# A clear of 96 columns behind each GpSimd scatter of edge columns, slots and node scores, in a two-layer graph transformer kernel

## The chip, the cores and the metric

The kernel runs on one core of one Trainium2 chip. The metric is the device time of one execution in microseconds, as the median of several runs. Three runs of the kernel before gave 2740.04, 2740.24 and 2740.77 us, a median of 2740.24 us.

## The reference

A graph of 3125 nodes with 256 features and 50,000 edges passes through two layers. Each layer adds a graph step, a token mixing step and a feed-forward step to the residual x. Cut to the steps that the change touches, in float32:

```python
# layer 0, graph step: weighted sum over the edges
support = layernorm(x) @ W                       # 3125 x 256
x += segment_sum(support[dst] * edge_weight[:, None], src, 3125) + bias   # plus linear attention

# layer 0, feed-forward: a shared network and 8 experts, two per node
x += gelu(xn @ W1s + b1s) @ W2s + b2s + sum_e gate[:, e] * expert_e(xn)

# layer 1: graph attention and linear attention, then 4 experts, whose gates come
# from a second graph attention over 32,768 edges given as another input
scores = mean_heads(layernorm(segment_softmax_sum(h[src2], dst2)))
x += sum_e softmax(top2(scores))[:, e] * (gelu(xn @ W1[e] + b1[e]) @ W2[e] + b2[e])
```

## The kernel before, in words

The nodes lie as 25 tiles of 125 rows. `self.x` holds the residual in SBUF throughout.

**Layer 0, graph step (`layer0_mix`).** The edges are turned into a dense adjacency matrix `adj` of 3125 by 3125 numbers in DRAM, and TensorE multiplies it with `sup`, the support. `adj` is zeroed by plain DMAs (`fill`, line 372). The edges are cut into 15 chunks of 128 rows and `WIDTHS` = 16, ten times 32, 24, 16, 8 and 7 columns, 391 columns in all. `edge_chunk` (line 322) computes on DVE the summed weight and the place of each edge of a chunk, and then issues one scatter a column (lines 350 to 355): an indirect DMA on GpSimd's queue, `scatter` at lines 56 to 60, which writes 128 single numbers to `adj`. Every scatter appears in the profile under line 58, so they are told apart by their tiles.

The product runs in eight runs of blocks of 125 rows of `adj` (`RUNS`, line 39: blocks 0-3, 4-7, 8-12, 13-16, 17-20, 21-22, 23 and 24). Each run first sees to it that the edge chunks that it needs have been issued (line 452), then loads its blocks into the tile `adjT`, of which five buffers exist (`load`, line 439, the DMAs at line 445, on SP's queue in an order written out by hand), and then, for each pair of node tiles, accumulates its blocks on TensorE (line 460) and adds the result to x on DVE (line 463). A pass of line 460 is one record of TensorE; each float32 product leaves two. Between the pairs, one step of a sort of the 32,768 edges of the last stage is taken (`next(sort, None)`, line 464); its work is on DVE and TensorE.

**Layer 0, feed-forward.** Each node's row of 264 numbers (features, two gates, two slots, its own number) is scattered twice into `slots` in DRAM, 50 scatters (lines 788 to 790). The shared network's layers follow (`hidden`, `output`), and then blocks of 256 slots are loaded (line 849) and sent through their experts.

**Layer 1, feed-forward.** The scores of each node for the second graph attention, five numbers a row in the tile `row`, are scattered into `starts` in DRAM, 25 scatters (lines 1685 and 1686). The tiles that come after, `y` among them (line 1706), lie in the memory of the pool that holds `row`. Then four experts run over seven chunks of nodes (lines 1724 to 1734), while GpSimd gathers the scores of the edges (`sources`, line 1696, gathers at line 51).

SP's queue within `layer0_mix` and DVE's within the last expert loop are ordered by hand; everything else is ordered by the framework's scheduler, which also sets the waits on semaphores.

Of the kernel before, what the change touches and what calls it, by code (L numbers as in the profile page):

```python
# [8 lines left out]
F32 = mybir.dt.float32  # L9
# [46 lines left out]
def scatter(nc, table, idx, rows, add=False):  # L56
    kw = {"compute_op": OP.add} if add else {}
    return nc.gpsimd.indirect_dma_start(  # L58
        out=table, out_offset=bass.IndirectOffsetOnAxis(ap=idx, axis=0),
        in_=rows, in_offset=None, **kw)  # L60


def move(queue, out, in_):


    for s in (slice(0, 112), slice(112, P)):
        queue.dma_start(out[s], in_[s])  # L67
# [7 lines left out]
def rows_of(table):  # L75
    return table.rearrange("(t p) d -> p t d", p=P)


def overlapping(ap, start, steps):

    return bass.AP(tensor=ap.tensor, offset=ap.offset + start,
                   ap=[list(ap.ap[0])] + [list(s) for s in steps])
# [6 lines left out]
class Kernel:  # L89
    def __init__(self, ctx, tc, a, out):  # L90
        self.tc, self.nc, self.a, self.out = tc, tc.nc, a, out
        self.const = ctx.enter_context(tc.tile_pool(name="const", bufs=1))
        self.dram = ctx.enter_context(tc.tile_pool(name="dram", bufs=1, space=DRAM))


    def constants(self):
        nc, a, c = self.nc, self.a, self.const
        self.x = c.tile([P, NT, D], F32, name="x")
        self.ident = c.tile([128, 128], F32, name="ident")
        make_identity(nc, self.ident)  # L100

        self.below = c.tile([128, 128], F32, name="below")
        nc.gpsimd.memset(self.below, 1.0)
        nc.gpsimd.affine_select(out=self.below, in_=self.below, compare_op=OP.is_gt, fill=0.0,
                                base=0, pattern=[[-1, 128]], channel_multiplier=1)

        self.above = c.tile([128, 128], F32, name="above")
        nc.gpsimd.memset(self.above, 1.0)
        nc.gpsimd.affine_select(out=self.above, in_=self.above, compare_op=OP.is_gt, fill=0.0,
                                base=0, pattern=[[1, 128]], channel_multiplier=-1)  # L110
        self.full = c.tile([128, 128], F32, name="full")
        nc.vector.memset(self.full, 1.0)

        self.spare = c.tile([128, 1], F32, name="spare")
        nc.gpsimd.iota(self.spare, pattern=[[0, 1]], base=N, channel_multiplier=1,
                       allow_small_or_imprecise_dtypes=True)
        self.node = c.tile([128, EC], F32, name="node")
        nc.gpsimd.iota(self.node, pattern=[[1, EC]], base=0, channel_multiplier=0,
                       allow_small_or_imprecise_dtypes=True)
        self.eps = c.tile([128, 1], F32, name="eps")  # L120
        nc.vector.memset(self.eps, LN_EPS)
        self.ones = c.tile([128, 1], F32, name="ones")
        nc.vector.memset(self.ones, 1.0)


        names = (("L0_ffn_b1s", 8), ("L0_ffn_b1p", 64), ("L1_ffn_b1", 16), ("L0_mix_g_pre", 2))
        total = sum(n for _, n in names)
        self.cols = c.tile([128, total], F32, name="cols")
        self.col_at = {}
        with self.tc.tile_pool(name="c_s", bufs=1) as sp, \  # L130
                self.tc.tile_pool(name="c_p", bufs=1, space=PSUM) as pp:
            st = sp.tile([total, 128], F32, name="c_st")
            r = 0
            for name, n in names:
                v = a[name]
                flat = bass.AP(tensor=v.tensor, offset=v.offset, ap=[[128, n], [1, 128]])
                nc.sync.dma_start(st[r:r + n, :], flat)
                self.col_at[name] = r
                r += n
            pt = pp.tile([128, total], F32, name="c_pt")  # L140
            nc.tensor.transpose(pt, st, self.ident[:total, :total])
            nc.vector.tensor_copy(self.cols, pt)
# [179 lines left out]
    def edge_chunk(self, pool, out, k, c, pieces):  # L322


        nc = self.nc
        e0 = 128 * sum(WIDTHS[:c])
        F, K = WIDTHS[c], HALO
        C, W = self.chunk_in[c]

        same = pool.tile([128, F + K, K], BF16, name="ch_same", bufs=1)  # L330
        nc.vector.tensor_tensor(same, C[:, :F + K, None].to_broadcast([128, F + K, K]),
                                overlapping(C, 1, [[1, F + K], [1, K]]), OP.is_equal)
        prod = pool.tile([128, F, K], F32, name="ch_prod", bufs=1)
        nc.vector.tensor_mul(prod, same[:, K:, :], overlapping(W, 1, [[1, F], [1, K]]))
        more = pool.tile([128, F], F32, name="ch_more")
        nc.vector.tensor_reduce(more, prod, AX.X, OP.add)
        wsum = out.tile([128, F], F32, name=f"ch_sum{c}")
        nc.vector.tensor_add(wsum, more, W[:, :F])

        dup = pool.tile([128, F], F32, name="ch_dup")  # L340
        flat = same.rearrange("p i k -> p (i k)")
        nc.vector.tensor_reduce(dup, overlapping(flat, K - 1, [[K, F], [K - 1, K]]), AX.X, OP.max)
        own = C[:, K:K + F]
        off = pool.tile([128, F], F32, name="ch_off")
        nc.vector.scalar_tensor_tensor(off, k[F], float(BEHIND + e0), own,
                                       op0=OP.add, op1=OP.subtract)
        nc.vector.scalar_tensor_tensor(off, dup, self.off, off, op0=OP.max, op1=OP.mult)
        place = out.tile([128, F], I32, name=f"ch_place{c}")
        nc.vector.tensor_add(place, off, own)
        for f in range(F):  # L350
            ins = scatter(nc, self.adj[:], place[:, f:f + 1], wsum[:, f:f + 1])
            self.tc.declare_no_dep(ins.ins, group="adj read", reason="blocks that are complete")
            for i in range(pieces, BEHIND // PIECE):
                self.tc.declare_no_dep(ins.ins, group=f"zeros {i}", reason="rows behind the chunk's")
            self.unordered("adj", ins)

    def layer0_mix(self):
        nc, tc, a = self.nc, self.tc, self.a
# [327 lines left out]
    def layer0_ffn(self):  # L686
        nc, tc, a = self.nc, self.tc, self.a
        NE, FC = 8, 8
        with ExitStack() as c:
# [98 lines left out]
            for t in range(NT):  # L788
                for i in range(2):
                    self.unordered("slots", scatter(nc, self.slots[:], abi[:, i, t:t + 1], rows[:, t, :]))  # L790

            gT = keep.tile([NE + 1, N], F32, name="gT")
            for t0, n in CHUNKS:
# [847 lines left out]
    def layer1_ffn(self):  # L1641
# [4 lines left out]
        with ExitStack() as c:  # L1646
# [18 lines left out]
            with tc.tile_pool(name="f1l", bufs=1) as lp:  # L1665
                rows = lp.tile([128, EC, 16], I32, name="s_back")
                nc.sync.dma_start(rows, self.sorted[:].rearrange("(p f) c -> p f c", p=128))
                nc.vector.tensor_copy(src, rows[:, :, 0])
                self.layernorm(lp, ps_a, "3", xT)


                ph = ps_a.tile([P, NT, 16], F32, name="ln_pt")
                for t in range(NT):
                    self.token_matmul(ph[:, t, :], xT, t, wgat)
                h = srow[:, :, 0:16]
                nc.vector.tensor_copy(h, ph)
                prod = lp.tile([P, NT, 16], F32, name="prod")
                row = lp.tile([P, NT, 5], F32, name="row0")
                nc.vector.memset(row, 1.0)
                for n, dest in (("att_src", srow[:, :, 16:20]), ("att_dst", row[:, :, 0:4])):  # L1680
                    nc.vector.tensor_mul(prod, h, vec[n][:, None, :].to_broadcast([P, NT, 16]))
                    nc.vector.tensor_reduce(dest, prod.rearrange("p t (h k) -> p t h k", h=4), AX.X, OP.add)
                move(nc.sync, rows_of(tabg[:]), srow)

                for t in range(NT):
                    self.unordered("starts", scatter(nc, self.starts[:], self.seg_at[:, 0, t:t + 1], row[:, t, :]))

                nc.vector.tensor_add(loop, srow[:, :, 16:20], row[:, :, 0:4])
                nc.vector.scalar_tensor_tensor(loop, loop, 0.2, loop, op0=OP.mult, op1=OP.max)
# [326 lines left out]
```

## Time and profile before

| What | Value |
|---|---|
| median of three runs | 2740.24 us |
| the profiled execution, its own time | 3120.83 us |
| its span | 3119.1 us |
| granted TensorE clock, mean | 0.843 |
| TensorE busy | 2254.7 us (72%) |
| DVE busy | 1500.3 us (48%) |
| ACT busy | 541.0 us (17%) |
| GpSimd busy | 1645.8 us (53%) |
| mean DMA traffic | 83 GB/s |

The profiled execution took 380.6 us longer than the median of the timed runs, so a duration in the profile may stand for less in a timed run. A group's line reads: line, engine, operation, output<-inputs, count, then busy time and mean nanoseconds of one, then the idle time of its engine just before it and what ended that. "remote" there means that the trace holds no event that explains the end of the wait, and "issue" that the engine waited for nothing that the profile shows. PE is TensorE, PEld its weight loads, POOL is GpSimd, and SPq is the queue of DMAs that SP issues. The rows of digits of the page cut the span into 40 slices of 78 us, each digit a busy share in tenths.

### The profile page before, as it was taken

How to read it: one execution, taken by the hardware profiler on the slowest of the kernel's cores; microseconds unless marked ns; L12 is line 12 of the kernel's file. 1: busy time of each engine (PE TensorE's matmuls, PEld its weight loads, DVE VectorE, ACT ScalarE, POOL GpSimd, SP SyncE). 2: the span in 40 equal slices, each digit the busy share in tenths (PEclk: the TensorE clock that was granted, in tenths of full speed). 3: DMA queues.
4: the chain of work that ended last, by engine and by line, in shares of the span. 5: the costliest groups of instructions: out<-in, count | busy, mean ns of one | idle time of the engine just before them, and what ended most of it. 6: DMA issues, size and time to landing. Idle time of an engine off the chain costs nothing. (4 is left out here: it accounts for less than half of the span.)

```text
span 3119.1 us, 26613 instructions
## 1 busy us (share of the span) xinstructions
PE 2254.7 (72%) x9047; PEld 1666.0 (53%) x9047; DVE 1500.3 (48%) x3575; ACT 541.0 (17%) x1104; POOL 1645.8 (53%) x1486
## 2 busy tenths in 40 slices
PE   1762652249999599879999859998777555868773
PEld 1441531138766556568888736665655443545552
DVE  7874940045556692112111168988777700212225
ACT  1420000000000121112222144443000200122213
POOL 5887877720000053256666537778777066655512
PEclk9855765569999599989999969999998667989886
DMA  8904310031233011335555252221222110112142
GB/s 308 379 12 94 83 21 1 0 81 41 60 81 102 29 54 42 115 109 184 187 182 175 98 149 48 47 47 45 48 49 49 61 36 7 22 35 47 38 97 69
DMA packets 175938, 259.80 MB, mean 83 GB/s; under 512 B 53839, under 2 KB 140857, under 8 KB 172402
## 3 DMA queue, kind: packets, MB, share of 16 engines
q1 hardware_dynamic: 117601, 201.63, 21.2%
q0 software_dynamic: 52288, 47.17, 7.1%
q10 hardware_dynamic: 5894, 9.09, 0.8%
q8 instruction: 76, 1.25, 0.2%
q14 instruction: 79, 0.65, 0.1%
HBM read 173.99 MB, written 83.69 MB: 83 GB/s over the span
## 5 line engine op out<-in xcount | busy, mean ns | idle before, releaser
L58 POOL DMA_INDIRECT adj<-ch_sum,ch_place x391 | 490.8, 1255 | 149.4 <-issue 121.8
L51 POOL DMA_INDIRECT g<-tab,t_src x391 | 460.9, 1179 | 119.4 <-issue 116.0
L460 PE MATMUL psum<-sup,adjT 125*125 125x256 f32 x1250 | 325.0, 409 | 225.4 <-issue 167.7
L460 PEld LDWEIGHTS psum<-sup,adjT 125*125 125x125 f32 x1250 | 249.2, 202 | 290.5 <-issue 197.9
L51 POOL DMA_INDIRECT G<-tabg,g_src x256 | 252.2, 985 | 159.4 <-DVE g_src L1701 83.7
L58 POOL DMA_INDIRECT sorted<-s_rows,pos x256 | 245.1, 957 | 172.8 <-DVE s_rows L1059 103.3
L1288 PE MATMUL pw<-v,hot 128*125 128x260 f32 x1244 | 305.4, 405 | 0.0
L1732 PE MATMUL fpy<-fw,fh 128*125 128x256 f32 x800 | 212.7, 423 | 94.8 <-ACT fh L1726 36.9
L1288 PEld LDWEIGHTS pw<-v,hot 128*125 128x125 f32 x1244 | 243.2, 199 | 43.3
L866 PE MATMUL ph<-xs,w 128*128 128x256 f32 x960 | 220.5, 388 | 49.6 <-issue 46.1
L1732 PEld LDWEIGHTS fpy<-fw,fh 128*125 128x125 f32 x800 | 165.9, 211 | 146.7 <-ACT fh L1726 45.0
L866 PEld LDWEIGHTS ph<-xs,w 128*128 128x128 f32 x960 | 183.4, 194 | 86.6 <-issue 57.6
L463 DVE TENSOR_TENSOR x<-x,psum 125x512 f32<-125x512 f32 (+1 forms) x104 | 68.8, 664 | 333.0 <-remote 224.3
L894 PE MATMUL py<-w,h 128*128 128x256 f32 x960 | 216.7, 379 | 0.0
L1724 PE MATMUL fph<-xT,fw 128*128 128x500 f32 (+1 forms) x448 | 181.3, 553 | 29.9 <-ACT fh L1726 25.7
L620 POOL MEMSET tier<- 125x64 f32 x1 | 0.2, 156 | 381.1 <-PE psum L460 381.1
L894 PEld LDWEIGHTS py<-w,h 128*128 128x128 f32 x960 | 180.2, 190 | 23.3
L868 ACT ACTIVATE h<-ph,b 128x256 f32<-128x256 f32 x240 | 113.1, 473 | 390.3 <-PE ph L866 293.6
L1034 PE MATMUL pctx<-s_mv,s_ro 128*128 128x256 f32 x512 | 154.7, 413 | 1.9 <-DVE s_mv L1033 1.9
L170 ACT ACTIVATE ln_rs<-ln_mv,eps 125x4 f32<-125x4 f32 (+1 forms) x21 | 5.5, 294 | 798.8 <-DVE ln_mv L169 798.8
L1726 ACT ACTIVATE fh<-fph,cols 128x500 f32<-128x500 f32 (+1 forms) x112 | 69.4, 632 | 420.8 <-PE fph L1724 236.2
L1724 PEld LDWEIGHTS fph<-xT,fw 128*128 128x128 f32 x448 | 85.7, 194 | 105.3 <-issue 53.8
(537 smaller groups left out, 3437.4 us busy)
## 6 DMA issues: line engine op xcount, KB each, us to landing
adjT<-adj SPq DMA_DIRECT2D x25, 1367.2 KB
adj<-zero SPq DMA_DIRECT2D x22, 1536.0 KB
w<-in_L_ffn_W1p_dram SPq DMA_DIRECT2D x30, 1024.0 KB
w<-in_L_ffn_W2p_dram SPq DMA_DIRECT2D x30, 1024.0 KB
slots<-empty SPq DMA_DIRECT2D x1, 8448.0 KB
srow<-slots SPq DMA_DIRECT2D x30, 264.0 KB
adj<-ch_sum,ch_place POOLq DMA_INDIRECT x391
g<-tab,t_src POOLq DMA_INDIRECT x391
```

Of the source, the lines that this page charges most:

```text
L51: nc.gpsimd.indirect_dma_start(out=out, out_offset=None, in_=table, in_offset=bass.IndirectOffsetOnAxis(ap=idx, axis=0))
L58: return nc.gpsimd.indirect_dma_start(out=table, out_offset=bass.IndirectOffsetOnAxis(ap=idx, axis=0), in_=rows, in_offset=None, **kw)
L460: nc.tensor.matmul(pm[:, i, :], mats[b][:, (a0 + i) * P:(a0 + i + 1) * P], sup[:, b, :], start=(b == b0), stop=(b == b0 + n - 1))
L463: nc.vector.tensor_add(xs, xs, pm[:, :m, :])
L866: nc.tensor.matmul(ph, w1[:, k, f * 128:(f + 1) * 128], xs[:, k, :], start=(k == 0), stop=(k == 1))
L868: nc.scalar.activation(h[:, f, :], ph, AF.Gelu, bias=b1[:, f:f + 1])
L894: nc.tensor.matmul(py, h[:, f, i * 128:(i + 1) * 128], w2[:, f, :], start=(f == 0), stop=(f == FC - 1))
L1034: nc.tensor.matmul(p1, ro[:, f - f0, :], mv, **st)
L1288: nc.tensor.matmul(pw.rearrange("p h c -> p (h c)"), hot[:, i - i0, :], v[:, i, :, :].rearrange("p h c -> p (h c)"), start=(i == i0), stop ...
L1724: nc.tensor.matmul(ph[:, :n * P], w1[:, k, f * 128:(f + 1) * 128], xT[:, k, t0 * P:(t0 + n) * P], start=(k == 0), stop=(k == 1))
L1726: nc.scalar.activation(hs[:, f, :n * P], ph[:, :n * P], AF.Gelu, bias=self.col("L1_ffn_b1", ei * FC + f))
L1732: nc.tensor.matmul(py, hs[:, f, i * P:(i + 1) * P], w2[:, f, :], start=(f == 0), stop=(f == FC - 1))
```

## The change

A tile `idle` of 128 partitions by 96 float32 is added to the constants. A new method clears it on GpSimd and asks the scheduler to keep the clear where it stands in the program. It is called behind each scatter to `adj`, `slots` and `starts`. Nothing reads the tile. The gathers, and the scatters of the sort and of the experts' outputs, get no clear.

```diff
+    def breath(self):
+
+        self.tc.keep_in_program_order(self.nc.gpsimd.memset(self.idle, 0.0))
+
...
         self.x = c.tile([P, NT, D], F32, name="x")
+        self.idle = c.tile([128, 96], F32, name="idle")
...
             for i in range(pieces, BEHIND // PIECE):
                 self.tc.declare_no_dep(ins.ins, group=f"zeros {i}", reason="rows behind the chunk's")
             self.unordered("adj", ins)
+            self.breath()
...
             for t in range(NT):
                 for i in range(2):
                     self.unordered("slots", scatter(nc, self.slots[:], abi[:, i, t:t + 1], rows[:, t, :]))
+                    self.breath()
...
                 for t in range(NT):
                     self.unordered("starts", scatter(nc, self.starts[:], self.seg_at[:, 0, t:t + 1], row[:, t, :]))
+                    self.breath()
```

## Prediction, made before the changed kernel was run

> **What bounds the kernel now.** I read four views in this order: the page's busy shares and groups, the waits of SP's DMA queue, GpSimd's timeline, and TensorE's timeline beside the waits of all engines.
>
> The change touches three groups of scatters, all issued by line 58. The page shows the first, the groups of GpSimd the other two (busy time and mean ns, then idle time before them and what ended it):
>
> ```profile
> span 3119.1 us, 26613 instructions
> ...
> POOL 5887877720000053256666537778777066655512
> ...
> L58 POOL DMA_INDIRECT adj<-ch_sum,ch_place x391 | 490.8, 1255 | 149.4 <-issue 121.8
> ```
>
> ```profile
> L58 POOL DMA_INDIRECT slots<-rows,abi x50 | 73.9, 1478 | 99.0 <-DVE r_cum L948 84.1 <-issue 14.9
> ...
> L58 POOL DMA_INDIRECT starts<-row,g_ati x25 | 29.5, 1180 | 56.1 <-DVE loop L1689 48.8 <-issue 7.3
> ```
>
> The 391 columns of adj fill GpSimd from 31 to 644 us (the first eight slices of its row). A column that nothing disturbs takes 0.96 us and starts 0.30 us after the end of the one before: 1.26 us a column.
>
> Whether this row of scatters bounds anything is told by who waits for it. Between 280 and 700 us SP's queue waited so:
>
> ```profile
> SPq L445 <- remote: 255.7, 1, 255.7
> SPq L445 <- DMA adj<-ch_sum,ch_place: 53.2, 1, 53.2
> ```
>
> Second row: one load of adjT, that of block 8, stood 53.2 us until column 208 had landed. The order of the program says why 208: the third run of the loop at line 450 (blocks 8 to 12) may read adj once 2000*13+560 = 26,560 edges are in, which takes chunks 0 to 6, 16+6*32 columns. Column 208 ends at 411.7 and the load goes out at 412.9. First row: the next load, block 9, then stood 255.7 us, until TensorE was through with blocks 4 to 7, whose buffers it needs. So in this execution TensorE, not GpSimd, held the third run. Its timeline shows how:
>
> ```profile
> 404.42 21.35 PE L460 MATMUL psum<-sup,adjT 125*125 125x256 f32 x92
> ...
> 466.83 0.58 PE L460 MATMUL psum<-sup,adjT 125*125 125x256 f32 x1 [2.22 <-issue]
> 469.63 0.58 PE L460 MATMUL psum<-sup,adjT 125*125 125x256 f32 x1 [2.22 <-issue]
> ```
>
> The 92 passes go at 0.232 us each; from 430 on they go at one per 2.80 us, with nothing that they wait for, until 670, shortly after the last column (644). The same engine sums up in the waits of all engines as:
>
> ```profile
> DVE x L463 <- remote: 224.3, 8, 41.9
> ACT fh L1726 <- remote: 113.6, 13, 50.0
> ```
>
> **Which of this is in the timed runs.** The profiled execution took 3120.83 us, 380.6 more than the median of 2740.24. Counting the records of line 460, 321 of the 400 passes of the first two runs stand before 425.8; the other 79 at 0.232 us would end at 444, and in the profile the second run ends at 671. That is 226 us; with the 113.6 us of the second row it makes 340 of the 380.6. Both stretches lie in an unbroken row of GpSimd DMAs with an idle DVE. I take it that the slow passes belong to the profiling and are absent from the timed runs. [...]
>
> Without the slow passes the second run ends at some 436 (444, less about 8 us of like waits at 278 to 302 us). Block 8's load takes 413.8 to 421.2, and blocks 9 to 12 need 27 us more from the end of the second run (670.2 to 697.5 in the profile). So column 208 has a slack of 436-421 = 15 us, or 23 if the 8 us stay: 19 in the middle. Later needs, from the spans of the runs in the profile (99, 91 and 83 us): the fourth run starts at about 535 and needs column 272 (493.7), the fifth at 626 and needs 336 (574.7), the sixth at 709 and needs 376 (625.4). GpSimd is nearly the bound of this stage, column 208 first.
>
> **The change part by part.** It adds 466 clears on GpSimd (391, 50 and 25) and one tile of 384 bytes a partition. The order of instructions on TensorE, DVE, ACT and SP is the same before and after, line by line; on GpSimd each clear stands right behind its scatter. From the second on a clear waits for the clear before it, which is done by then. Queued behind a clear is the next scatter and, through it, SP's load.
>
> *What a clear costs.* Nearest rows: a clear of 128 columns is busy 0.194 to 0.204 us and of 64 columns 0.156; halfway, 96 columns: 0.178. In a row of clears the starts are closer (0.81 and 0.95 for two of 128 columns: 0.14 us), so 96 cost 0.115 where they overlap. What stands directly behind a DMA shows in one place:
>
> ```profile
> 2631.46 0.94 POOL L51 DMA_INDIRECT G<-tabg,g_src  x1 [0.30 <-issue]
> 2632.42 0.14 POOL L1764 IOTA g_part<- 128x1 f32 x1
> 2635.22 0.95 POOL L51 DMA_INDIRECT G<-tabg,g_src  x1 [2.65 <-DVE g_src L1701]
> ```
>
> The iota starts 0.02 us after the DMA ends, so the 0.30 us is not a pause that follows every DMA: it belongs to the start of the next one. Whether a clear falls into it or pushes it back is not shown, as the DMA behind this iota waits for DVE. Bounds: 0 (it fits in the 0.30), and 0.02+0.178+0.30 = 0.50 (a second such start). I take the middle of 0.115 and 0.20, that is 0.16 us, with the start pushed back whole[...]. If the clear also waits for DVE as the scatters do (1255-960 = 0.30 us a column), its share by duration is 0.05 more; a clear reads nothing, so I leave that out.
>
> [...]
>
> *adj (391).* 208*0.16 = 33 us for column 208, less 19 of slack: the third run 14 us later. Fourth: column 272 at 493.7+43.5 = 537 against 535+14: no more. Fifth: column 336 at 628.5, with up to 20 us of DVE's hold on GpSimd that the timed runs have here and the profile has not (DVE idle), against 640: 0 to 8, I take 4. Sixth: column 376 at 686 against 727: nothing. Sum 18 us. [...]
>
> *slots (50).* 8 us more on a row that ends at 1205.3; the first load of slots goes out at 1293.5. Hidden behind 88 us of the shared network's hidden layers and the sort; without that cover 8 us.
>
> *starts (25).* In the chain of waits: scatters from 2509.4 to 2546, then DVE's `y` (39.0 us waiting for `DMA starts<-row,g_ati`), while TensorE stands 25.7 us for DVE. Nothing covers it: 25*0.16 = 4 us.
>
> Total +22 us: 2740.24+22 = 2762. [...] On the profiled execution's own time the same sum would be 3121 plus 4 if its slow passes stay as they are, since they hide adj; I expect that its time moves by far more, either way, with the length of these passes, and do not use it.
>
> **The rivals.**
> *The clear hides in the 0.30 us* (not slower; 12%). For: the start of a DMA could be prepared while the clear runs. Against: the gap is the same for DMAs of 0.94 and 1.18 us, as if serial. It decides if the price is under about 0.05 us a column: 208*0.05 = 10 is inside the slack, 25*0.05 = 1. Time 2741.
> *The scatters bind throughout* (slower; 10%): the clear costs 0.50. Third run 104-19 = 85 late; fourth at 493.7+136 = 630 against 620, 95; fifth at 574.7+168 = 743 against 721, 117; starts 12.5. Time 2740+130 = 2870; at half of it 2790.
> *The slow passes are in the timed runs too, and the clears free TensorE* (faster; 8%). For: TensorE recovers whenever GpSimd's row breaks. Against: the 380.6 us would then have to come from elsewhere. All of it: 2740-226+22 = 2536.
>
> **How the numbers follow.** Clear in series, slack near 19: 70%, 2762, with 2746 to 2790 from prices of 0.115 to 0.20 and slacks of 0 to 24. The range takes in the hidden clear and the lower half of the third case: 2740 to 2800; it leaves out the gain (8%) and about 9% above. A measurement here can tell about 0.2%, 5.5 us. Slower: 67 of the 70 and 10: 77%. Same: 12 and 3, less one that falls either way: 14%. Faster: 9%.
>
> **What would show it.** In the profile after: clears of 0.16 to 0.20 us; scatter to scatter 1.42 us where it was 1.26 (1.26 would be the first rival, 1.7 the second); starts' 25 scatters 4 us longer; SP's load of block 8 issued near 446 instead of 413. TensorE's passes at 2.80 us, if they shorten while the median does not fall, are the profiling's own. A median under 2735 would make my reading of the slow passes wrong; one over 2800, the slack or the price.

## The result, and the profile after

| Kernel | Median, runs | Range |
|---|---|---|
| before | 2740.14 us, 9 runs | 2734.98 to 2742.60 |
| after | 2747.68 us, 9 runs | 2744.68 to 2751.55 |

The ratio is 1.003, with a 95% interval of 1.002 to 1.004: 7.5 us slower. The forecast was +22 us (2762). The direction held and the size was a third of it. Ratios here and below are estimated from the runs within 1.5% of their kernel's fastest, which leaves 11 of the 22 runs of e5, so they need not be the quotient of the two medians. The profiled execution of after took 2747.69 us, in a span of 2745.9 us at a granted clock of 0.887, so this profile stands for the timed runs, as the profile of before (3120.83 us) did not. The experiments ran in four sets, each beside the kernel before on one chip. One set, e5 to e8, met a chip where the kernel before itself took 3107.7 us with the slow TensorE passes of its first profile.

The page of after, where the rows shown of before stood:

```profile
span 2745.9 us, 27078 instructions
...
POOL 5999898886000822666666267778777407777751
...
L58 POOL DMA_INDIRECT adj<-ch_sum,ch_place x391 | 491.0, 1256 | 93.4 <-issue 64.7
```

The groups of GpSimd in after (busy time and mean ns, then the idle time before them):

```profile
L97 POOL MEMSET idle<- 128x96 f32 x466 | 93.5, 201 | 0.3
L58 POOL DMA_INDIRECT slots<-rows,abi x50 | 71.7, 1434 | 94.6 <-DVE r_cum L955 85.4 <-issue 9.2
...
L58 POOL DMA_INDIRECT starts<-row,g_ati x25 | 29.6, 1184 | 53.6 <-DVE loop L1697 49.1 <-issue 4.5
```

The clears are there, 466 of 0.201 us, 93.5 us in sum. The column to read against before is the last one. The pauses before adj's scatters that nothing explains fell from 121.8 to 64.7 us, those before slots from 14.9 to 9.2, and those before starts from 7.3 to 4.5. So the clears came partly out of pauses that were there before (e1 below, a profile of before without its slow passes, has 110.9 us before adj's scatters). GpSimd's timeline of after shows one column:

```profile
560.28 0.96 POOL L58 DMA_INDIRECT adj<-ch_sum,ch_place  x1 [0.17 <-issue]
561.24 0.19 POOL L97 MEMSET idle<- 128x96 f32 x1
561.60 0.96 POOL L58 DMA_INDIRECT adj<-ch_sum,ch_place  x1 [0.17 <-issue]
```

The clear stands directly behind its scatter, and the next scatter starts 0.17 us after the clear, where it started 0.30 us after a scatter in before. From start to start it is 1.32 us, against 1.26. A clear of 0.20 us costs 0.06.

TensorE's slow passes are gone. In its timeline the stretch that began at 404 in before runs through the end of the second run of blocks without a break:

```profile
404.36 41.61 PE L466 MATMUL psum<-sup,adjT 125*125 125x256 f32 x182
446.23 0.70 PE L466 MATMUL psum<-sup,adjT 125*125 125x256 f32 x2 [0.26 <-DVE x L469]
```

SP's queue waited so in after, between 280 and 760 us (sum, times, longest):

```profile
SPq L451 <- PE psum L466: 225.9, 5, 61.8
SPq L451 <- DMA adj<-ch_sum,ch_place: 191.0, 5, 53.9
```

The second row is the one that had a single wait of 53.2 us in before, for column 208. Now it has five, so the same row must be taken apart by time. The waits of SP between 200 and 320 us show the one that matters:

```profile
SPq L451 <- DMA adj<-ch_sum,ch_place: 24.7, 1, 24.7
```

That is the very first load of adjT. SP came to it at 260.4 and could send it at 285.1. TensorE's timeline shows what hung on it:

```profile
263.21 0.59 PE L1176 MATMUL ln_pt<-attnT,w_nat 64*128 64x4 f32 x2
295.00 3.75 PE L466 MATMUL psum<-sup,adjT 125*125 125x256 f32 x8 [31.21 <-DMA adjT<-adj]
```

TensorE stood 31.21 us for this load. The prediction did not count this wait, and it turned out to be the place where adj's clears enter the time.

**The revised theory (T1).** Which column does the first load wait for? Blocks 0 to 3 need 80 columns, and the 80th ended at 171.9 us. But `edges(4)` and `edges(5)` (lines 528 and 568 of the kernel before), in the linear attention, have already issued chunks 3 and 4 by then, so 144 columns stand ahead of the load in the program. The traces fit that number: column 144 ended at 283.9 us in after and the load went out at 285.1, and the same 1.2 us lie between the two in the first profile of before and in e1 to e4, e9, e10, e13 and e14. The theory: a clear costs 0.06 us; it counts for columns 0 to 143, which have no slack, and for the 25 scatters to starts, and nowhere else.

**Rivals.** T2: the prediction's place, column 208 with 19 us of slack and then column 336. T3: each clear costs the same wherever it stands. T4: starts and slots carry the difference.

### The profile page after: what moved, and what is told of

The parts are those of the page before. It is cut to its first block, busy times and chain, and to the rows that moved or that the text cites. A ratio compares the mean times of both kernels' runs of the same rounds, so it can differ in the third digit from the quotient of the medians.

```text
span 2745.9 us, 27078 instructions
## 1 busy us (share of the span) xinstructions
PE 2185.3 (80%) x9047; PEld 1644.0 (60%) x9047; DVE 1500.3 (55%) x3575; ACT 542.2 (20%) x1104; POOL 1737.0 (63%) x1952
## 5 line engine op out<-in xcount | busy, mean ns | idle before, releaser
L58 POOL DMA_INDIRECT adj<-ch_sum,ch_place x391 | 491.0, 1256 | 93.4 <-issue 64.7
L466 PE MATMUL psum<-sup,adjT 125*125 125x256 f32 x1250 | 292.5, 393 | 53.2 <-DMA adjT<-adj 41.8
L466 PEld LDWEIGHTS psum<-sup,adjT 125*125 125x125 f32 x1250 | 240.6, 194 | 94.7 <-DMA adjT<-adj 31.3
L1740 PE MATMUL fpy<-fw,fh 128*125 128x256 f32 x800 | 184.3, 386 | 35.9 <-DVE y L1742 30.9
L1740 PEld LDWEIGHTS fpy<-fw,fh 128*125 128x125 f32 x800 | 151.0, 191 | 73.3 <-DVE y L1742 32.5
L1732 PE MATMUL fph<-xT,fw 128*128 128x500 f32 (+1 forms) x448 | 174.9, 540 | 0.2 <-DMA fw<-in_L_ffn_W_dram 0.2
L904 DVE TENSOR_SCALAR yo<-py,own 128x256 f32<-128x256 f32 x60 | 27.8, 481 | 192.2 <-PE py L901 192.2
L58 POOL DMA_INDIRECT slots<-rows,abi x50 | 71.7, 1434 | 94.6 <-DVE r_cum L955 85.4
```

Source lines behind the costliest of these rows:

```text
L58: return nc.gpsimd.indirect_dma_start(out=table, out_offset=bass.IndirectOffsetOnAxis(ap=idx, axis=0), in_=rows, in_offset=None, **kw)
L466: nc.tensor.matmul(pm[:, i, :], mats[b][:, (a0 + i) * P:(a0 + i + 1) * P], sup[:, b, :], start=(b == b0), stop=(b == b0 + n - 1))
L1732: nc.tensor.matmul(ph[:, :n * P], w1[:, k, f * 128:(f + 1) * 128], xT[:, k, t0 * P:(t0 + n) * P], start=(k == 0), stop=(k == 1))
L1740: nc.tensor.matmul(py, hs[:, f, i * P:(i + 1) * P], w2[:, f, :], start=(f == 0), stop=(f == FC - 1))
```

## The experiments

All ran beside the kernel before on the same chip. "Before" in the tables is its median there.

### e1: the kernel before, profiled again

No edit.

> The kernel before, unchanged, profiled once more, for stage times without the slow TensorE passes. If the slow passes (one per 2.80 us) belong to one profiled execution, this profile is near 2740 us, and the first load of adjT goes out near 261-264 us plus the wait for column 144, which ends near 277-283: TensorE idle some 20-25 us there, where the first profile hid it behind slow passes. If the passes belong to the kernel, the profile takes about 3120 us again. Scatter to scatter 1.26 us, gap 0.30 us.

One run, 2741.59 us. Its page, and its TensorE waits between 200 and 760 us:

```profile
span 2739.8 us, 26613 instructions
...
L58 POOL DMA_INDIRECT adj<-ch_sum,ch_place x391 | 512.8, 1311 | 150.3 <-issue 110.9
```

```profile
PE psum L460 <- DMA adjT<-adj: 40.7, 4, 29.7
```

and SP's queue, with the first load of adjT:

```profile
284.01 4.06 SPq L445 DMA_DIRECT2D adjT<-adj  x8
```

The same program, profiled, took 379 us less than in its first profile (2741.59 against 3120.83). TensorE waits 29.7 us for the first load of adjT, which went out at 284.0; in the first profile that wait was 9.17 us, since TensorE itself came late, at 284.8. The mean scatter is longer here (1311 ns against 1255). In the first profile DVE was busy for 23.4 of the 240 us from 430 to 670, beside TensorE's slow passes; here it works in those stretches (4, 6 and 5 tenths in its row of e1's page from 479 to 685 us), and some scatters beside DVE take longer: of e1's 391, the 84 with no DVE instruction beside them took at most 0.962 us each, and 74 of the other 307 over 1.2 us. In the first profile the longest ends at 81.44 us, behind two DVE instructions that follow each other from 70.72 to 80.60, of which the first and the scatter itself are:

```profile
70.72 6.81 DVE L521 TENSOR_TENSOR x<-x,xn 125x6400 f32<-125x6400 f32 x1
70.76 10.68 POOL L58 DMA_INDIRECT adj<-ch_sum,ch_place  x1 [0.31 <-issue]
```

Such stretches are called DVE's holds below; what makes these scatters long was not shown.

### e2 to e4: where the clears count

The clears split by place. e2 has the call in `edge_chunk` alone, e3 has the two others alone, and e4 has this:

```diff
             self.unordered("adj", ins)
-            self.breath()
+            if c < 5:
+                self.breath()
```

with the clears behind slots and starts taken out.

> Clears behind the 391 scatters to adj alone. Theory T1 (a clear costs about 0.06 us a column, since the start of the next scatter shrinks from 0.30 to 0.17 us; on the path are columns 0-143, for which the first load waits, and nothing later): 144*0.06 = 8.6 us less what DVE's holds swallow, about +6, 2746. Theory T2 (the place of the prediction, column 208 with 19 us of slack): 208*0.06 = 12.5, inside the slack, 0, so 2740. Theory T4 (starts and slots carry the difference): 0, 2740.

> Clears behind the 50 scatters to slots and the 25 to starts, none at adj. T1: slots hidden, starts 25*0.06 = 1.5 us, so 2741.5. T2: the same 1.5 us. T4 (starts and slots carry the difference): +7, 2747.

> Clears behind the scatters of chunks 0 to 4 alone, columns 0 to 143. T1: all that adj costs is here, about +6, 2746. T2 (column 208 with slack, 144*0.06 = 8.6 inside 19 us): 0, 2740. T3 (each clear costs the same wherever it stands, 7.5 us over 466): 144/466 of 7.5 = +2.3, 2742.5.

| Kernel | Median | Before | Ratio, 95% |
|---|---|---|---|
| e2, adj alone | 2749.82 | 2738.88 | 1.004 (1.0026 to 1.0054) |
| e3, slots and starts | 2740.11 | 2738.88 | 1.0008 (1.0000 to 1.0016) |
| e4, columns 0 to 143 | 2746.88 | 2738.88 | 1.0026 (1.0011 to 1.0041) |

T4 falls: slots and starts together cost 1.2 us (0 to 4). T2 falls: with clears behind columns 0 to 143 alone it expected nothing, and 8.0 us (3 to 11) came. e2 came out at 10.9 us (7 to 15), above the 6 of T1 and above the changed kernel itself (7.5), which has more clears. The intervals of the two overlap; what else is in e2's 10.9 is open. In its profile, of a run of 2742.11 us, the first load went out at 287.0.

### e5 to e8: the same questions on another chip

e5 has clears from column 144 on (`if c >= 5:`). e6 is e4 with a tile three times as wide:

```diff
-        self.idle = c.tile([128, 96], F32, name="idle")
+        self.idle = c.tile([128, 288], F32, name="idle")
```

e7 has no clears. `edge_chunk` hands its scatters back as a function, and those of chunks 3 and 4 are called behind the first loads. In the program the first load then stands behind 80 columns instead of 144:

```diff
-                        self.edge_chunk(ch, keep, number, chunk, -(-tiles * P * N // PIECE))
+                        scatters = self.edge_chunk(ch, keep, number, chunk, -(-tiles * P * N // PIECE))
+                        if chunk in (3, 4):
+                            held.append(scatters)
+                        else:
+                            scatters()
...
                 load(b0 + n)
+                while held:
+                    held.pop(0)()
```

e8 is e7 with all 466 clears.

> Clears behind the scatters of chunks 5 to 14 alone, columns 144 to 390. T1 (only columns 0 to 143 lie on the path): at most 1 us, 2739 to 2741. T2 (column 208, then 336, bind, as in the prediction): 64*0.06 to 192*0.06, 4 to 11 us, 2743 to 2750. T3 (every clear costs the same wherever it stands, 7.5 us over 466): 247/466 of 7.5 = +4, 2743.

> The clears of 144 columns, each over 288 numbers a partition instead of 96. From 0.156 us for 64 and 0.20 for 128 columns a clear of 288 should be busy some 0.35 us, 0.15 to 0.17 more than 0.20. T1 (columns 0 to 143 stand on the path without slack, and what a clear takes beyond the 0.13 us that it saves in the gap goes into the end): 144*(0.06+0.16) = about +32, 2771. T2 (column 208 with 19 us of slack): 32-19 = +13, 2752. If a clear runs beside the start of the next scatter whatever its length, no more than +8.

> No clears. The scatters of chunks 3 and 4 (columns 80 to 143) are issued in the program behind the first run's loads, so that these wait for column 80 and not for 144; the order on every engine is the same as before, only that wait differs. T1: the first load goes out at 261 us instead of 284, TensorE's wait of 30 us shrinks to about 7, and column 208 (410) is then next: -20 to -23, 2717. T2 (the first load isn't on the path; column 208 with slack): 0, 2740.

> As in e7, and all 466 clears. T1: column 80 is far ahead of the first load (172 against 261), so the clears cost nothing there; the second run then ends near 421, and column 208 with its load has next to no slack: 0 to 6 us, and 1.5 of starts, over e7: 2718 to 2725. T3 (7.5 us wherever they stand): 7.5 over e7.

| Kernel | Median | Before | Ratio, 95% |
|---|---|---|---|
| e5, columns 144 to 390 | 3084.40 | 3107.70 | 0.9842 (0.981 to 0.9875) |
| e6, wide clears | 3133.96 | 3107.70 | 1.010 (1.0061 to 1.0138) |
| e7, earlier loads | 3109.67 | 3107.70 | 1.001 (0.9994 to 1.0025) |
| e8, earlier loads and clears | 3083.45 | 3107.70 | 0.9928 (0.9894 to 0.9962) |

None of the expectations was made for this. e7 brought nothing, where T1 expected 20 to 23 us less; e6 cost 26 us by the medians, where T1 expected 32. The kernel before took 3084 to 3170 us in all its 49 timed runs here, and the profiles show the passes at one per 2.80 us again, here TensorE's timeline of e7:

```profile
464.42 0.59 PE L469 MATMUL psum<-sup,adjT 125*125 125x256 f32 x1 [2.21 <-issue]
467.22 0.59 PE L469 MATMUL psum<-sup,adjT 125*125 125x256 f32 x1 [2.21 <-issue]
```

So these passes are not the work of one profiled execution. The reason that the prediction gave for leaving them out, that they belong to the profiling, was the author's estimate and does not hold as it stands, though the runs of the comparison had none. On this chip kernels with clears behind column 143 were faster: by the medians e5 23 us and e8 24, and e8, which differs from e7 by the clears alone, 26 us faster than e7. TensorE's waits between 280 and 700 us, first of e7 and then of e8:

```profile
PE psum L469 <- issue: 180.4, 89, 2.9
```

```profile
PE psum L475 <- issue: 59.6, 44, 11.8
```

With clears behind the scatters, the pauses in these passes that nothing explains shrink from 180.4 us to 59.6. This is the effect that the prediction's third rival named, TensorE freed by clears, seen on a chip that has these passes, though most of it does not reach the end: pass 400 of the product starts at 494 us in e8 and at 641 in e7, but pass 650, near the end of the third run, at 752 and 774. (e5's profile is of its fastest run, 3038.49 us, and differs from the others before any clear, with its first load at 315.1 us, so it is not used here.) What makes the slow passes, and whether they belong to the chip or to the time at which it was used, no run here shows.

### e9 to e12: the four kernels again, where the kernel before takes 2740 us

> The kernel of e5 once more, since e5 to e8 ran where the kernel before itself took 3108 us, with slow TensorE passes in its timed runs; the numbers hold for a chip on which it takes 2740. T1 (only columns 0 to 143 lie on the path): at most 1 us more than before. T2 (column 208, then 336): +4 to +11. T3 (every clear costs the same): +4. If this chip has the slow passes too: some 1.6% less than before, as in e5.

> The kernel of e6 once more (clears of 144 columns over 288 numbers a partition). T1: what a clear takes beyond the 0.13 us that the gap gives back goes whole into the end: +32. T2 (19 us of slack): +13. If a clear runs beside the start of the next scatter whatever its length: no more than +8.

> The kernel of e7 once more (no clears; the first loads wait for column 80 instead of 144). T1, where the kernel before takes 2740: -20 to -23. T2: 0. With slow passes they hide it, as in e7: 0.

> The kernel of e8 once more (first loads wait for column 80, all 466 clears). T1, where the kernel before takes 2740: 1.5 to 7 over e11. T3 (7.5 us wherever the clears stand): 7.5 over e11. With slow passes: some 0.7% under the kernel before, as in e8.

| Kernel | Median | Before | Ratio, 95% |
|---|---|---|---|
| e9, columns 144 to 390 | 2737.85 | 2739.86 | 0.9998 (0.999 to 1.0006) |
| e10, wide clears | 2764.87 | 2739.86 | 1.010 (1.0085 to 1.0115) |
| e11, earlier loads | 2718.09 | 2739.86 | 0.9922 (0.9909 to 0.9934) |
| e12, earlier loads and clears | 2721.49 | 2739.86 | 0.9939 (0.9926 to 0.9952) |

e9: 247 clears behind column 143 cost nothing (at most 1.6 us), where T2 expected 4 to 11 and T3 4. Both fall. In its profile column 208 ended at 403.9 and block 8's load went out at 405.1, while TensorE was busy with the second run until 441.

e10 measures the price. GpSimd's timeline:

```profile
271.90 0.96 POOL L58 DMA_INDIRECT adj<-ch_sum,ch_place  x1 [0.17 <-issue]
272.86 0.35 POOL L97 MEMSET idle<- 128x288 f32 x1
273.37 0.96 POOL L58 DMA_INDIRECT adj<-ch_sum,ch_place  x1 [0.17 <-issue]
```

The clear is longer by 0.16 us, and the pause behind it is the same 0.17. A median column steps on by 1.482 us instead of 1.266: the price is 0.216, which is the clear (0.352, median) less 0.14. Over 144 columns that is 31 us. The 144 columns took 277.1 us instead of 250 (27 us; where the other 4 went was not shown). Its waits of SP (200 to 320 us) and of TensorE (200 to 760 us):

```profile
SPq L452 <- DMA adj<-ch_sum,ch_place: 42.8, 1, 42.8
```

```profile
PE psum L467 <- DMA adjT<-adj: 60.9, 4, 49.6
```

The first load went out at 309.6 us, 25.5 after that of e1; TensorE's wait for it is 19.9 us longer than in e1, and began 5.6 us later. The kernel took 25.0 us more (23 to 32 by the interval), so nearly every microsecond of column 144 goes into the end. The profiles together say the same: in after, e1 to e4, e9, e10, e13 and e14 the first load goes out at anything from 280.0 to 309.6 us, and from there to the end of the execution it is 2454 to 2463 us in all nine. T2's 13 us is outside.

e11 takes the other way to the same place; its trace has the instructions of every engine in the same order as e1's. SP's row from 200 to 320 us in e11, the queue's timeline, and TensorE's waits:

```profile
SPq L452 <- DMA adj<-ch_sum,ch_place: 15.1, 1, 15.1
```

```profile
259.70 4.07 SPq L452 DMA_DIRECT2D adjT<-adj  x8
```

```profile
PE psum L469 <- DMA adjT<-adj: 17.8, 4, 7.2
```

The first load goes out at 259.7 us instead of 284.0, without waiting; the 15.1 us now stand before block 4's load at 291.5. TensorE's longest wait for a load falls from 29.7 to 7.2 us, and the kernel is 21.8 us faster. It beats both kernels of this case.

e12 lies 3.4 us over e11, as T1 has it (1.5 to 7). The two intervals overlap, so e12 alone would not exclude T3's 7.5.

### e13 and e14: a clear of one column, and the changed kernel again

```diff
-        self.idle = c.tile([128, 96], F32, name="idle")
+        self.idle = c.tile([128, 1], F32, name="idle")
```

> All 466 clears, each over 1 number a partition instead of 96. Behind clears of 96 and of 288 numbers alike the next scatter starts after 0.165 us instead of 0.305, so a clear gives 0.14 us back. If that is so for any clear, one of 0.06 to 0.14 us (an iota of one column took 0.14) costs nothing or less: scatter to scatter 1.19 to 1.27 us, column 144 as early as before, and -3 to +1 us over the kernel before. If the 0.14 us comes back only beside a long enough clear: step 1.32 or more, and +5 to +8 as with 96.

> The changed kernel itself once more, beside e13 on the same chip. Where the kernel before takes 2740: +7, column 144 at 284 to 288. If this chip is one with slow TensorE passes (the kernel before near 3108): the clears shorten the passes that run beside adj's scatters, as e5 and e8 (-23 to -49 us) suggest, and the change makes the kernel faster, by 0.7 to 1.6%; if the gain in e5 had another cause, slower by 6 or the same.

| Kernel | Median | Before | Ratio, 95% |
|---|---|---|---|
| e13, clears of one column | 2740.93 | 2739.60 | 1.0007 (0.9998 to 1.0016) |
| e14, after again | 2748.75 | 2739.60 | 1.0035 (1.0022 to 1.0048) |

The groups of GpSimd in e13:

```profile
L58 POOL DMA_INDIRECT adj<-ch_sum,ch_place x391 | 513.6, 1314 | 101.4 <-issue 62.9 <-DMA ch_w<-in_edge_weight_dram 26.7 <-DMA adj<-ch_sum,ch_place 5.8
...
L97 POOL MEMSET idle<- 128x1 f32 x466 | 59.0, 127 | 0.3
```

Its timeline of GpSimd:

```profile
558.94 0.96 POOL L58 DMA_INDIRECT adj<-ch_sum,ch_place  x1
559.90 0.12 POOL L97 MEMSET idle<- 128x1 f32 x1
560.20 1.07 POOL L58 DMA_INDIRECT adj<-ch_sum,ch_place  x1 [0.19 <-issue]
```

466 clears of 0.127 us, 59.0 us of new work in GpSimd's row, cost nothing that can be told (at most 4 us). The median clear of 0.118 us and the pause of 0.191 behind it make 0.309, the old pause of 0.305. The median step is 1.265 us, and column 144 ended at 282.8, where it did in e1. So it is the length of the clear that costs, and not that an instruction stands there. e14 met a chip without the slow passes, so what the whole change does where they are was not seen: e8 beside e7 speaks for a gain there, and no run of the changed kernel itself shows it.

The pauses and steps of adj's columns, medians from the traces, tell the price in one table:

| Clear | Its time | Pause behind it | Step | Price |
|---|---|---|---|---|
| none (e1) | | 0.305 | 1.266 | |
| 1 column (e13) | 0.118 | 0.191 | 1.265 | 0 |
| 96 columns (after) | 0.195 | 0.165 | 1.322 | 0.06 |
| 288 columns (e10) | 0.352 | 0.165 | 1.482 | 0.22 |

## Why the prediction was wrong in size

**The price of a clear (0.16 us) failed.** The step took the clear "with the start pushed back whole", which was the author's estimate. The start is not pushed back whole: the pause of 0.305 us before a scatter is 0.165 us behind a clear of 96 or 288 columns, as if 0.14 of it went on while the clear runs. So the price is the clear less 0.14: 0.06, and nothing for the clear of 0.118 us. The clear itself was sized well, 0.178 from the rows against 0.195 measured. The first rival, "the start of a DMA could be prepared while the clear runs", came out for nearly half of the pause (0.14 of 0.305 us); the prediction weighed it as all or nothing. What makes the pause shorter behind a clear, no run here shows.

**The place (column 208 with 19 us of slack) failed.** That column had more slack: in e1 its load went out at 411.8 and the second run ended near 445. The bound was column 144, with none. The prediction had the sign of it in hand, "about 8 us of like waits at 278 to 302 us", took it for slow passes and subtracted it: 436 from 444, where the second run ended at 445 in e1. What stands there in the first profile is this wait:

```profile
293.96 3.75 PE L460 MATMUL psum<-sup,adjT 125*125 125x256 f32 x8 [9.17 <-DMA adjT<-adj]
```

TensorE waited 9.17 us for the first load, and it waits 29.7 us where it is not late itself (e1). What would have told is the program: the first load waits for what was issued before it, not for what its blocks need.

**The sum.** Predicted: adj 18, slots 0, starts 4. The two errors worked against each other, and the direction of adj's part came out right by luck: with its right price at its own place, adj would have cost nothing.

- *adj.* 144 columns at 0.06 make 8.6 us. In the profiles columns 0 to 143 took 250.1 us in the mean without clears (e1, e3, e9, e11: 247.9 to 252.0) and 256.3 with them (after, e2, e4, e12, e14: 253.2 to 259.0): 6.2. One pair of profiles would not tell it, as after alone is 1.2 us over e1. With the predicted price at the right place it would have been 144*0.16 = 23; with the right price at the predicted place, 208*0.06 = 12.5, nothing at all.
- *The fifth run's 4 us* did not come: e9 has every later clear and costs nothing. Two things cover them. The later runs have slack (36 us at block 8's load in e9, 405.1 against 441). And columns 144 to 390 hardly take longer: 382.4 us in the mean without clears there (e1, e3, e4, e10, e11, e13) and 385.0 with clears of 96 columns (after, e2, e9, e12, e14), where 247*0.06 would make 15, since the scatters there are shorter with clears between them (1.18 us in the mean in e9, 1.23 in e1). The 20 us of DVE's holds in the step were right: column 336 ended at 593.7 us in e1 and at 574.7 in the first profile, 19.0 us apart.
- *slots*, 0, was right: the row ended at 984.0 us and took 90.7 instead of 89.2 (e1), behind the cover that was named; e3 shows no more than starts.
- *starts* had the right place and 1.85 us instead of 4: 38.7 us from first to last in after, against 36.85 in e1. DVE's wait for them, in before and in after:

```profile
DVE y L1734 <- DMA starts<-row,g_ati: 39.0, 1, 39.0
```

```profile
DVE y L1742 <- DMA starts<-row,g_ati: 40.9, 1, 40.9
```

6.2 and 1.85 make 8.0, where 7.5 (after) and 9.2 (e14) were measured.

**The signs that were named.** Clears of 0.16 to 0.20 us: 0.20. A step of 1.42 us: 1.32, between the first rival's 1.26 and that. starts 4 us longer: 1.85. Block 8's load near 446: it went out at 409.0 in after, while the second run lasted to 446, so it bound nothing.

**The slow passes.** That they were absent from the timed runs was right, and it carried the forecast away from the third rival. The reason, the author's estimate from 340 of the 380.6 us, was wrong as it stands: on one chip all 49 timed runs of the kernel before took 3084 to 3170 us, about what its first profile took (e5 to e8), and on another a profile of it had no slow passes (e1). That 340 of 380.6 us fit could not tell such a condition from the profiling's own cost. Gaps between the scatters did bring time there, 26 us (e8 beside e7), though far less than 226. Whether the profiling has any part in the passes was not shown.

**The rivals.** The hidden clear (2741) is ruled out by the interval, though 0.14 us of each clear of 96 columns did not show in the step. Scatters binding throughout at 0.50 us (2870) fell with e9 and with the step of 1.32. TensorE freed by clears did not happen in the comparison; e8 beside e7 shows it on the chip with slow passes.

## What to carry to other kernels

Find the wait that ends last from the program as well as from the profile: here a load waited for all 144 scatters issued before it, though its blocks needed 80, and in one profile another delay covered most of that wait. Issuing 64 of them after the load was worth 21.8 us (e11). A small instruction between two indirect DMAs of GpSimd cost, here, what it took beyond 0.14 us, so measure the step from start to start and not the instruction. Where a profile takes far longer than the timed runs (here 3120.83 us against 2740.14), profile again before building on any duration in it.

## What the runs showed of the hardware

- The pause before an indirect DMA of 128 numbers was 0.305 us behind another one (e1), and 0.165 us behind a clear of 96 (after) or of 288 columns (e10), 0.14 us less. A clear of 0.118 us and the pause behind it together took 0.309 us (e13).
- A clear on GpSimd took 0.118, 0.195 and 0.352 us (medians) for 1, 96 and 288 columns of 128 partitions (e13, after, e10): by these three about 0.8 ns more for each column.
- Of 391 such DMAs in e1, the 84 with no DVE instruction beside them took at most 0.962 us each; 74 of the other 307 took over 1.2 us, the longest 10.69.
- On one chip the kernel before took 3084 to 3170 us in all 49 timed runs, against 2731 to 2745 on three others, at a granted clock of 0.834 to 0.851 against 0.884 to 0.890. The profiles there show TensorE's passes at one per 2.80 us beside GpSimd's scatters. Clears between the scatters brought TensorE's unexplained pauses there from 180.4 us (e7) down to 59.6 (e8), and the time down by 26 us. The cause is open.
